# Graph network on one core: the first gather of a tile waits for the scores of the tile three places ahead, in layers 1 and 3

## Chip, cores and metric

The kernel runs on one core of one Trainium2 chip. The metric is the device time of one execution in microseconds (us), as the median of several runs. PE is TensorE, DVE VectorE, ACT ScalarE, POOL GpSimd, SP SyncE; a DMA that gathers rows is issued by POOL.

## What is computed

Four layers over a graph of N = 2048 nodes, with B = 8 batches of D = 64 features. Every layer normalises `x`, clips it at zero, lets every node attend to its neighbours in `adj`, and adds the result to `x`. Layers 1 and 3 are the ones that the change touches; both score an edge by a sum of one number of each end:

```python
def _L3_gnn_ref(x, adj, W, a):
    h = jnp.matmul(x, W)
    a1 = a[:F_out, 0]
    a2 = a[F_out:, 0]
    f1 = jnp.einsum('bnf,f->bn', h, a1)
    f2 = jnp.einsum('bnf,f->bn', h, a2)
    e = jax.nn.leaky_relu(f1[:, :, None] + f2[:, None, :], negative_slope=ALPHA)
    e = jnp.where(adj[None, :, :] > 0, e, NEG_BIG)
    attention = jax.nn.softmax(e, axis=2)
    h_prime = jnp.matmul(attention, h)
    return jax.nn.relu(h_prime)
...
    # --- layer 3 (adj_preln) ---
    h = jnp.maximum(_layernorm(x, axis=-1), 0.0)
    x = x + _L3_gnn_ref(h, adj, L3_gnn_W, L3_gnn_a)
```

Layer 1 is the same with `elu` in place of `relu` at its end. Layer 0 scores with dot products, layer 2 with dot products in two passes (four heads, then one).

## The kernel before

The graph is sparse: a node has few neighbours, and node 0 the most. In layer 0 the kernel builds edge lists from `adj`. The nodes lie in 16 tiles of 128, T0 to T15. A tile has some slots of 128 edges: `ROWS` slots in which partition p holds an edge of node p, and `PACKED` slots in which edges lie in any order and are assigned to nodes by a selection matrix on PE. Together they are 17 for T0, 8 for T1, 6 for T2, 5 for T3 to T5, 4 for T6 to T10 and 3 for T11 to T15, 81 in all.

A slot is filled by `gather(k, i, st)`: one indirect DMA from POOL takes 128 rows of `table[k]` (512 features and, in layers 1 and 3, 8 numbers `f2` behind them, 2080 bytes a row, 266 KB a slot) into one slot of `ring`, which has `RING = 26` slots of SBUF. A slot is free again when the products with it have been made. A gather thus waits for its slot of the ring, and for one of eight DMA semaphores in turn, the one that the gather eight places before it set.

`additive(k, wd, ...)` runs layer 1 (k = 1, tiles in `ORDER1`) and layer 3 (k = 4, tiles in `ORDER`). Its steps run as a pipeline over the tiles, so that a step of one tile stands beside later steps of tiles ahead of it:

- `take`: the gathers of the tile.
- `sums` (layer 3 alone): exponentials (ACT, L507) and their sums, from which a shift `fs` for each node comes.
- `first`: the scores. `by_edge` brings the node's own number to packed edges (PE), DVE adds it to the gathered number (L532, L535), `leaky` (DVE, L448) ends the scores, ACT takes the exponential (L542), DVE copies it (L544).
- `check`: `by_query` sums the weights by node (PE L399, DVE L403), `weigh_sum` multiplies the ring's slots by the weights (DVE or POOL, L380) and sums them on PE (L385); this frees the slots.
- `third`, `project` and the end: division (DVE L465), transposition (PE L306, ACT L307), product with the weight matrix (PE L561), then in layer 1 `elu` (ACT L570 and L571, DVE L572), the sum with `x` (L473), and the norm for the next layer (DVE L267 to L288, POOL L290 and L292), in layer 3 `relu` and the sum (DVE L906) and the store.

Tiles come in these orders:

```python
ORDER1 = [13, 14, 15, 12, 11, 10, 0, 7, 6, 1, 5, 2, 4, 3, 9, 8]
ORDER = [13, 12, 11, 10, 9, 8, 0, 7, 6, 1, 5, 2, 4, 3, 14, 15]
```

Semaphores are set by the framework from what instructions read and write. A scheduler at build time decides the order of the instructions on each engine from estimated times and from these dependences; on the chip, each engine then runs its own list in that order. In layer 3 all gathers stand on POOL in one row with nothing between them; in layer 1 some of the norm's instructions stand between.

Of the kernel before, what the change touches and what calls it, by code (L numbers as in the profile page):

```python
# [1 line left out]

# [11 lines left out]
OP = mybir.AluOpType  # L14
# [4 lines left out]
SLOPE = 0.2  # L19
# [15 lines left out]

PAIRS = [0, 0, 2, 2, 2, 0, 0, 0, 2, 2, 2, 2, 2, 2, 2, 2]
QE = 4


MAKING = [15, 14, 13, 0, 12, 11, 10, 1, 9, 2, 8, 3, 7, 4, 6, 5]  # L40
# [19 lines left out]
def edge_stack(ctx: ExitStack, tc: tile.TileContext, x_in, adj, w1, w1t, a1, wh, wht, bh, wo, bo,  # L60
# [9 lines left out]
    nc = tc.nc  # L70
# [52 lines left out]
    def slots(t, i):  # L123
        return t[:, OFF[i]:OFF[i] + SLOTS[i]]
# [87 lines left out]
    order = list(MAKING)  # L212

    def pipeline(*stages):

        states = {}
        for n in range(NT + len(stages) - 1):
            for s in reversed(range(len(stages))):
                if 0 <= n - s < NT:
                    i = order[n - s]  # L220
                    stages[s](i, states.setdefault(i, {}))
# [4 lines left out]
    def tiny(n):  # L226

        at = spot[0] if spot[0] + n <= F else 0
        spot[0] = at + n
        return bank[0][:, at:at + n]  # L230
# [3 lines left out]
    def rows(i, lo, hi, most=RING):  # L234

        t = lo
        while t < hi:
            at = (held[i] + t) % RING
            m = min(most, hi - t, RING - at)
            yield t, m, ring[:, at:at + m, :]  # L240
            t += m
# [1 line left out]
    def row(i, t):  # L243
        return ring[:, (held[i] + t) % RING, :F]

    def gather(k, i, st):

        n = SLOTS[i]
        assert sum(SLOTS[j] for j in held) + n <= RING
        held[i], front[0] = front[0], (front[0] + n) % RING  # L250
        cols = table[k].shape[1]
        for t in range(n):
            nc.gpsimd.indirect_dma_start(  # L253
                out=ring[:, (held[i] + t) % RING, :cols], out_offset=None, in_=table[k][:, :],
                in_offset=bass.IndirectOffsetOnAxis(ap=idx[:, OFF[i] + t:OFF[i] + t + 1], axis=0))

    def load(st, name, src, bufs):
        st[name] = rows_pool[0].tile([P, F], F32, name=name, bufs=bufs)
        nc.sync.dma_start(out=st[name], in_=src)
# [41 lines left out]
    def transposed(src):  # L301

        t = rows_pool[0].tile([P, F // P, P], F32, name="xt", bufs=3)
        p = ps_q.tile([P, F], F32, name="q")
        for k in range(F // P):
            nc.tensor.transpose(p[:, k * P:(k + 1) * P], src[:, k * P:(k + 1) * P], ident)  # L306
        nc.scalar.copy(t.rearrange("p k n -> p (k n)"), p)  # L307
        return t
# [83 lines left out]
    def by_query(i, w, cols):  # L392


        K, T = ROWS[i], PACKED[i]
        w, packed = w if isinstance(w, list) else (w[:, :K, :], w[:, K:, :])
        p = (thin[0] or ps_m).tile([P, F], F32, name="m")
        for t in range(T):
            nc.tensor.matmul(p[:, :cols], selt(i, t), packed[:, t, :], start=(t == 0), stop=(t == T - 1))  # L399
        if K == 1:  # L400
            return w[:, 0, :], p[:, :cols]
        d = small.tile([P, cols], F32, name=f"row{cols}")
        nc.vector.tensor_reduce(d, w.rearrange("p k c -> p c k"), AX.X, OP.add)  # L403
        return d, p[:, :cols]

    def by_edge(i, v, cols):

        T = PACKED[i]
        p = (thin[0] or ps_m).tile([P, F], F32, name="m")
        pv = p[:, :T * cols].rearrange("p (t c) -> p t c", t=T)  # L410
        for t in range(T):
            nc.tensor.matmul(pv[:, t, :], sel(i, t), v, start=True, stop=True)
        return pv
# [31 lines left out]
            nc.vector.tensor_tensor(dst, p, u, op=OP.max)  # L445

    def leaky(dst, src):
        nc.vector.scalar_tensor_tensor(dst, src, SLOPE, src, op0=OP.mult, op1=OP.max)  # L448


    def first0(i, st):
# [3 lines left out]
    def second(i, st, wp=None):  # L455
        w = slots(w_all, i)
        d, p = by_query(i, w, B)
        st["rec"] = small.tile([P, B], F32, name="rec")
        nc.vector.tensor_tensor(st["rec"], p, d, op=OP.add)
        nc.vector.reciprocal(st["rec"], st["rec"])  # L460
        st["y"] = weigh_sum(i, st, w) if wp is None else weigh_sum(i, st, wp, eng=nc.vector)
        done(i, st)

    def divide(st, dst):
        nc.vector.tensor_tensor(heads(dst), heads(st["y"]), wide(st["rec"]), op=OP.mult)  # L465
# [11 lines left out]
    def take0(i, st):  # L477
        gather(0, i, st)
        load(st, "rows", rows_of(0, i), 3)
# [6 lines left out]
    def both(*fs):  # L486
        def f(i, st):
            for g in fs:
                g(i, st)
        return f  # L490
# [8 lines left out]

    def additive(k, wd, *finish):  # L500
        def take(i, st):
            gather(k, i, st)

        def sums(i, st):
            w = slots(w_all, i)
            for t, m, g in rows(i, 0, SLOTS[i]):
                nc.scalar.activation(w[:, t:t + m], g[:, :, F:], AF.Exp, scale=1.0 / TEMP)  # L507
            d, p = by_query(i, w, B)
            S = small.tile([P, B], F32, name="S")
            nc.vector.tensor_tensor(S, p, d, op=OP.add)  # L510
            nc.vector.tensor_reduce(most[:, 1, i:i + 1], S, AX.X, OP.max)
            nc.vector.tensor_reduce(least[:, 1, i:i + 1], S, AX.X, OP.min)

            z = small.tile([P, B], F32, name="z")
            nc.vector.tensor_scalar(z, S.bitcast(I32), TEMP * LN2 / 2 ** 23, -127.0 * TEMP * LN2, op0=OP.mult,
                                    op1=OP.add)
            nc.vector.tensor_tensor(z, z, f1s[:, i, :], op=OP.add)
            st["fs"] = small.tile([P, 2, B], F32, name="fs")
            nc.scalar.copy(st["fs"][:, 0, :], f1s[:, i, :])
            leaky(st["fs"][:, 1, :], z)  # L520

        def first(i, st):
            K, T = ROWS[i], PACKED[i]
            w = slots(w_all, i)
            s = slots(s_all, i)
            fs = st["fs"].rearrange("p t b -> p (t b)") if k == 4 else f1s[:, i, :]
            n = 2 * B if k == 4 else B
            pr = tiny(2 * B)
            nc.vector.tensor_copy(pr[:, :n], fs)
            pv = by_edge(i, fs, n)  # L530
            for t, m, g in rows(i, 0, K):
                nc.vector.tensor_tensor(s[:, t:t + m, :], g[:, :, F:], pr[:, None, :B].to_broadcast([P, m, B]),  # L532
                                        op=OP.add)
            for t, m, g in rows(i, K, K + T):
                nc.vector.tensor_tensor(s[:, t:t + m, :], g[:, :, F:], pv[:, t - K:t - K + m, :B], op=OP.add)  # L535
            leaky(s, s)
            if k == 4:
                nc.vector.tensor_tensor(s[:, :K, :], s[:, :K, :], pr[:, None, B:].to_broadcast([P, K, B]),
                                        op=OP.subtract)
                nc.vector.tensor_tensor(s[:, K:, :], s[:, K:, :], pv[:, :, B:], op=OP.subtract)  # L540
                nc.vector.tensor_scalar(s, s, 60.0, None, op0=OP.min)
            nc.scalar.activation(w, s, AF.Exp)  # L542
            wp = tiny((K + T) * B)
            nc.vector.tensor_copy(wp, w.rearrange("p t b -> p (t b)"))  # L544
            st["wp"] = wp.rearrange("p (t b) -> p t b", b=B)

        def check(i, st):
            second(i, st, st["wp"])
            if k == 1:
                nc.vector.tensor_reduce(most[:, 0, i:i + 1], st["rec"], AX.X, OP.max)  # L550
                nc.vector.tensor_reduce(least[:, 0, i:i + 1], st["rec"], AX.X, OP.min)

        def third(i, st):
            st["att"] = rows_pool[0].tile([P, F], F32, name="att")
            divide(st, st["att"])
            st["xt"] = transposed(st["att"])

        def project(i, st):
            p = st["p"] = ps_q.tile([P, F], F32, name="q")
            for j in range(F // P):  # L560
                nc.tensor.matmul(p[:, j * P:(j + 1) * P], st["xt"][:, j, :], wd, start=True, stop=True)  # L561
            finish[0](i, st)

        mid = [sums] if k == 4 else []
        pipeline(take, *mid, first, both(check, xs_rows), third, project, *finish[1:])
# [148 lines left out]
    with tc.tile_pool(name="l2", bufs=2) as l2p, \  # L714
# [10 lines left out]
        def fetch(upto):  # L725

            while len(sent) <= min(upto, len(stream) - 1):
                i, t = stream[len(sent)]
                q = sent[i, t] = l2p.tile([P, QW], F32, name="qe", bufs=QE)
                nc.gpsimd.indirect_dma_start(  # L730
# [3 lines left out]
        def take2(i, st):  # L734
# [4 lines left out]
            else:  # L739
                st["q"] = own_pool[0].tile([P, QW], F32, name="q")  # L740
                nc.sync.dma_start(out=st["q"], in_=qtab[i * P:(i + 1) * P, :])
            fetch(stream.index((i, 0)) + min(PACKED[i], QE) - 1)

        def score(i, st, lo, hi):
# [5 lines left out]
            for t in range(lo, hi):  # L750
# [11 lines left out]
                if t >= K:  # L762
                    fetch(stream.index((i, t - K)) + QE)

# [675 lines left out]
```

## Time and profile before

| | us |
|---|---|
| median of 3 runs | 1672.45 (1670.03 to 1676.54) |
| the profiled execution | 1721.51 |
| its span, first to last instruction | 1719.7 |
| layer 1, first gather to last gather's start | 402.5 to 540.4 |
| layer 3, first gather to last gather's start | 1529.0 to 1670.2 |
| busy in the span: DVE | 1318.4 (77%) |
| busy in the span: PE | 1215.1 (71%) |
| busy in the span: POOL | 1153.4 (67%) |
| busy in the span: ACT | 744.5 (43%) |

The profiled execution took 2.9% more than the median; times inside a stage come from it alone. A line of the profile's groups has the line of the kernel, the engine and operation, output and inputs with their shapes, the count, then busy time, mean duration of one (ns), and the idle time just before with what ended it. "issue" as a releaser means that the engine waited for nothing that the profile shows, "remote" that the semaphore's sender isn't in the profile's reckoning. A timeline's line has start, duration, engine, line and operation, and in brackets the idle time before it with its releaser.

### The profile page before, as it was taken

Reading aid. Unit: us, or ns where it says so; the run is one execution under the profiler, and the core shown is the slowest. Engines: PE = TensorE matmul, PEld = TensorE weight load, DVE = VectorE, ACT = ScalarE, POOL = GpSimd, SP = SyncE. Lnnn points to the kernel's source line nnn. Section 1 sums busy time; section 2 is a strip of 40 time slices with the busy share of each in tenths; the row PEclk is TensorE's granted clock in tenths of the full one; section 3 lists DMA queues with packets and bytes.
Section 4 is the critical chain, followed back from the end, with each engine's and each line's share of the span. In section 5 each row is a group of like instructions: output and inputs, shape, how many; then the busy total and the mean of one; then the engine's idle time right before and its main releaser. Section 6 shows DMA issues by size and latency. Waiting matters only on the chain.

```text
span 1719.7 us, 15784 instructions
## 1 busy us (share of the span) xinstructions
PE 1215.1 (71%) x3771; PEld 606.6 (35%) x3771; DVE 1318.4 (77%) x2748; ACT 744.5 (43%) x2378; POOL 1153.4 (67%) x903
## 2 busy tenths in 40 slices
PE   0025667776479974599997999999467877555877
PEld 0002334443234431234342444443223433333545
DVE  6979999992469987699997899831389889823656
ACT  5841324441146783356531545545234445620011
POOL 5766867786554125898789889985577896654540
PEclk9998876896699997799999999999787879657989
DMA  5555454455566447656255345200643542235651
GB/s 172 167 182 179 152 200 153 141 198 156 147 201 235 158 179 260 233 189 208 87 201 200 113 157 177 87 13 19 255 141 99 154 146 70 81 119 164 197 170 51
DMA packets 85787, 266.94 MB, mean 155 GB/s; under 512 B 14627, under 2 KB 14659, under 8 KB 75446
## 3 DMA queue, kind: packets, MB, share of 16 engines
q0 software_dynamic: 37328, 141.05, 26.7%
q1 hardware_dynamic: 48358, 124.79, 20.4%
q8 instruction: 32, 0.52, 0.1%
q14 instruction: 69, 0.57, 0.1%
HBM read 208.74 MB, written 57.05 MB: 155 GB/s over the span
## 4 chain that ended last, share of the span: by engine, by line
PE 25%; POOL 11%; DVE 9%; issue 7%; ACT 5%; DMA 3%; another core or an unknown queue 2%; DVEq 0%; SPq 0%; POOLq 0%; ACTq 0%
PE y L787 10%; PE y L385 4%; POOL g L253 3%; POOL wh L772 3%; PE m L836 2%; ACT yn L795 2%; PE m L824 2%; PE y L779 2%; POOL wg L380 1%; DMA g<-table,idx 1%; POOL ln_r L290 1%; DMA rows<-table 1%; PE m L399 1%; DVE prod L755 1%
## 5 line engine op out<-in xcount | busy, mean ns | idle before, releaser
L253 POOL DMA_INDIRECT g<-table,idx x405 | 399.2, 986 | 233.5 <-issue 161.7
L772 POOL TENSOR_TENSOR wh<-g,w 128x1024 f32<-128x1024 f32 x162 | 307.5, 1918 | 30.0 <-PE y L787 28.0
L385 PE MATMUL y<-wg,ident 128*128 128x512 f32 x392 | 234.5, 729 | 72.7 <-POOL wg L380 64.3
L290 POOL TENSOR_TENSOR ln_r<-ln_q,mhalf 128x8 f32<-128x8 f32 x80 | 135.8, 1701 | 160.6 <-DVE ln_q L288 85.1
L759 DVE TENSOR_REDUCE s<-prod 128x32 f32<-128x2048 f32 x81 | 184.0, 2286 | 14.8 <-ACT w L761 12.9
L380 POOL TENSOR_TENSOR wg<-g,w 128x1024 f32<-128x1024 f32 (+1 forms) x91 | 158.9, 1756 | 37.3 <-ACT w L436 24.2
L787 PE MATMUL y<-wh,ident 128*128 128x512 f32 x320 | 154.6, 610 | 28.9 <-POOL wh L785 25.1
L385 PE MATMUL y<-wg,selt 128*128 128x512 f32 x256 | 141.6, 663 | 5.4 <-POOL wg L380 4.4
L385 PEld LDWEIGHTS y<-wg,ident 128*128 128x128 f32 x392 | 81.6, 228 | 162.2 <-POOL wg L380 78.9
L787 PE MATMUL y<-wh,selt 128*128 128x512 f32 x256 | 124.7, 614 | 10.4 <-POOL wh L772 10.4
L795 ACT ACTIVATE yn<-y,rec 128x64 f32<-128x64 f32 x512 | 111.2, 368 | 27.5 <-PE y L787 26.9
L755 DVE TENSOR_TENSOR prod<-q,g 128x2048 f32<-128x2048 f32 x49 | 111.5, 2276 | 5.3 <-ACT g L753 4.6
L399 PE MATMUL m<-w,selt 128*128 128x8 f32 (+1 forms) x384 | 59.5, 258 | 76.0 <-ACT w L542 38.2
L380 DVE TENSOR_TENSOR wg<-g,tiny 128x1024 f32<-128x1024 f32 (+1 forms) x92 | 98.2, 1086 | 17.1 <-PE y L385 8.8
L399 PEld LDWEIGHTS m<-w,selt 128*128 128x128 f32 x384 | 63.5, 213 | 122.3 <-ACT w L542 43.6
L442 DVE SCALAR_TENSOR_TENSOR zt<-m,bhc,att 128x512 f32<-128x512 f32 x64 | 47.3, 738 | 75.0 <-ACT att L441 74.4
L298 ACT ACTIVATE xh<-x,ln_r 128x64 f32<-128x64 f32 x256 | 88.3, 428 | 18.8 <-POOL ln_r L292 18.7
L787 PEld LDWEIGHTS y<-wh,ident 128*128 128x128 f32 x320 | 59.0, 193 | 104.9 <-issue 63.8
L428 PE MATMUL q<-rows,sel 128*128 128x512 f32 x128 | 84.3, 762 | 15.7 <-DVE prod L422 5.0
L753 ACT COPY g<-g 128x512 f32<-128x512 f32 x81 | 50.4, 622 | 100.5 <-DVE prod L755 87.9
L755 DVE TENSOR_TENSOR prod<-qe,g 128x2048 f32<-128x2048 f32 x32 | 73.0, 2282 | 17.0 <-DMA qe<-qtab,qidx 15.9
L779 PE MATMUL y<-rows,ident 128*128 128x512 f32 x128 | 70.0, 634 | 18.3 <-DMA rows<-table 13.6
(210 smaller groups left out, 2584.7 us busy)
## 6 DMA issues: line engine op xcount, KB each, us to landing
qtab<-q SPq DMA_DIRECT2D x16, 1040.0 KB
a<-in_adj_dram SPq DMA_DIRECT2D x16, 1024.0 KB
q<-qtab SPq DMA_DIRECT2D x14, 1040.0 KB
table<-xh SPq DMA_DIRECT2D x48, 256.0 KB
rows<-table SPq DMA_DIRECT2D x48, 256.0 KB
xs<-x SPq DMA_DIRECT2D x48, 256.0 KB
x<-xs SPq DMA_DIRECT2D x48, 256.0 KB
table<-xh SPq DMA_DIRECT2D x32, 260.0 KB
```

The lines of the kernel that those rows point to most:

```text
L253: nc.gpsimd.indirect_dma_start(out=ring[:, (held[i] + t) % RING, :cols], out_offset=None, in_=table[k][:, :], in_offset=bass.IndirectOffse ...
L290: nc.gpsimd.tensor_tensor(st["rstd"][:, 0, :], q, mhalf, op=OP.pow)
L298: nc.scalar.activation(dst[:, b * D:(b + 1) * D], st["src"][:, b * D:(b + 1) * D], func, bias=0.0 if st["less"] is None else r[:, 1, b:b + ...
L380: eng.tensor_tensor(wg[:, :m].rearrange("p t (b d) -> p t b d", b=B), g[:, :, :F].rearrange("p t (b d) -> p t b d", b=B), w[:, t0:t0 + m, ...
L385: nc.tensor.matmul(y, lhs(i, t), wg[:, t - t0, :], start=(t == 0 and own is None), stop=(t == n - 1))
L399: nc.tensor.matmul(p[:, :cols], selt(i, t), packed[:, t, :], start=(t == 0), stop=(t == T - 1))
L755: nc.vector.tensor_tensor(pr.rearrange("p (b h) d -> p b h d", h=H), q[:, :B * H * D].rearrange("p (b h d) -> p b h d", h=H, d=D), heads(g ...
L759: nc.vector.tensor_reduce(s[:, t - lo, :], pr, AX.X, OP.add)
L772: nc.gpsimd.tensor_tensor(wg, heads(row(i, t))[:, :, None, :].to_broadcast([P, B, 2, D]), w[:, :, 2 * k:2 * k + 2, None].to_broadcast([P, ...
L779: nc.tensor.matmul(st["ys"][j], ident, xb[:, 4 * j:4 * j + 4], start=True, stop=False)
L787: nc.tensor.matmul(st["ys"][j], lhs(i, t), wg[:, 4 * j:4 * j + 4], start=False, stop=(t == n - 1))
L795: nc.scalar.activation(yn[:, b, h, :], st["ys"][j][:, b, h, :], AF.Copy, scale=st["rec"][:, 4 * j + b, 2 * k + h:2 * k + h + 1])
```

## The change

A dictionary `taken` keeps, for each layer and tile, the instruction that ends the tile's scores (`leaky(s, s)` in `first`). `take` hands to `gather` the one of the tile three places ahead in the layer's order, and `gather` makes it a dependence with a semaphore, of the tile's first slot (t = 0) alone. The first three tiles of each layer have none. In layer 0 and layer 2 `gather` is called as before.

```diff
+SPREAD = 3
...
-    def gather(k, i, st):
+    taken = {}
+
+    def gather(k, i, st, behind=None):
...
         for t in range(n):
-            nc.gpsimd.indirect_dma_start(
+            g = nc.gpsimd.indirect_dma_start(
                 out=ring[:, (held[i] + t) % RING, :cols], out_offset=None, in_=table[k][:, :],
                 in_offset=bass.IndirectOffsetOnAxis(ap=idx[:, OFF[i] + t:OFF[i] + t + 1], axis=0))
+            if behind is not None and t == 0:
+                tc.add_manual_dep(g.ins, behind.ins.name, mybir.DependencyInfo(
+                    mybir.DependencyClass.Sync, mybir.DependencyReason.DATA), reason="gather")
...
     def leaky(dst, src):
-        nc.vector.scalar_tensor_tensor(dst, src, SLOPE, src, op0=OP.mult, op1=OP.max)
+        return nc.vector.scalar_tensor_tensor(dst, src, SLOPE, src, op0=OP.mult, op1=OP.max)
...
         def take(i, st):
-            gather(k, i, st)
+            n = order.index(i)
+            gather(k, i, st, taken[k, order[n - SPREAD]] if n >= SPREAD else None)
...
-            leaky(s, s)
+            taken[k, i] = leaky(s, s)
```

An import that nothing uses is left out here. The lines of the kernel after are shifted: by 4 at the gather (L253 becomes L257), by 7 from the norm to `leaky` (L290 becomes L297, L448 becomes L455), by 8 behind that (L507 becomes L515).

More of the change, by code (lines that the diff above doesn't have):

```diff
@@ L1 @@
-from contextlib import ExitStack
+from contextlib import ExitStack, nullcontext
 import concourse.bass as bass
```

## The prediction

> **What bounds the kernel now.** I read the page's chain and costliest groups first, then the waits of the two stages that the change touches, then their engines one by one in time.
>
> ```profile
> PE 25%; POOL 11%; DVE 9%; issue 7%; ACT 5%; DMA 3%; another core or an unknown queue 2%; DVEq 0%; SPq 0%; POOLq 0%; ACTq 0%
> L253 POOL DMA_INDIRECT g<-table,idx x405 | 399.2, 986 | 233.5 <-issue 161.7
> ```
>
> No engine holds the whole span. A gather costs POOL 0.99 us, and about 1.25 us from one start to the next (below), so the 81 gathers of a layer need 101 us. The layers last longer: layer 1 from 402.5 to about 660, layer 3 from 1529.0 to 1715. In layer 1 the stretches say what binds (columns: stretch, length, then busy time of PE, PEld, DVE, ACT, POOL, then clock, DMA share, GB/s):
>
> ```profile
> 400.00:450.00 50.00, 15.31 (x50) 8.62 (x49) 10.93 (x42) 1.25 (x4) 33.27 (x35) 0.64 0.66 187
> 450.00:500.00 50.00, 36.77 (x135) 21.33 (x136) 29.79 (x71) 18.31 (x55) 27.79 (x29) 0.85 0.55 162
> 500.00:600.00 100.00, 93.96 (x348) 49.36 (x346) 93.97 (x211) 71.61 (x199) 35.17 (x37) 1.00 0.56 199
> ```
>
> Up to 450 only POOL works hard: it issues 35 gathers in an unbroken stream. From 500 DVE and PE are 94% busy, so the layer is bound by them and not by gathers: the last gather starts at 540.4, the scores of the last tile come at 590.4. The waits of 400 to 560 tell why the start is empty (waiter, releaser, total us, times, longest):
>
> ```profile
> ACT e L570 <- remote: 44.4, 2, 29.5
> ...
> POOL g L253 <- DVE wg L380: 22.5, 4, 9.1
> POOL g L253 <- issue: 20.4, 70, 0.3
> ```
>
> ACT waited 29.5 us for a semaphore whose sender the profile can't name; in the trace it is PE's, for matmuls recorded as ended 25 us before. On POOL and DVE at that place (start, duration, what ended the idle time):
>
> ```profile
> 445.20 0.95 POOL L253 DMA_INDIRECT g<-table,idx  x1 [0.30 <-issue]
> 455.21 0.95 POOL L253 DMA_INDIRECT g<-table,idx  x1 [9.06 <-DVE wg L380]
> ```
>
> ```profile
> 434.83 0.17 DVE L448 SCALAR_TENSOR_TENSOR s<-s 128x24 f32<-128x24 f32 x1
> 452.39 0.70 DVE L572 SCALAR_TENSOR_TENSOR q<-q,e 128x512 f32<-128x512 f32 x1 [17.38 <-ACT e L571]
> ```
>
> The stream stops at 446.15 because the ring is full, PE's updates come at 451.1, and DVE goes on at 452.39. Layer 3 repeats it: the stream stops at 1568.94, and DVE goes on at 1573.45 after this wait (1525 to 1720):
>
> ```profile
> ACT w L507 <- DMA g<-table,idx: 59.6, 12, 14.5
> ...
> DVE x L906 <- remote: 13.3, 1, 13.3
> ```
>
> From then on layer 3 too runs behind its gathers: the last one starts at 1670.2, and the scores of its tile come at 1704.8.
>
> **What the skill says.** The Trainium skill, "DMA: Bandwidth & Descriptors", Anatomy of one DMA, says that DMA engines don't wait on semaphores; the wait is on the issuing sequencer. The trace agrees: POOL's own row shows the 9.06 us. So a gather that waits holds back every later gather, and every norm (L290) queued on POOL. The same page, Issuing engines are not separate DMA queues, says that DMAs from all engines share the same 16 DMA engines; a stopped gather stream thus leaves room to others. The trace shows 187 GB/s in the stream, and doesn't show anybody served sooner. "Perfetto Trace Analysis", Tensor Engine Instruction, says that TensorE's recorded end is an estimate: the 25 us between recorded end and update may therefore be work that really ended late.
>
> **The change part by part.** Both kernels have the same gathers, bytes and arithmetic. Only a tile's first slot (t = 0) gets the new wait; slots 1 and up have none, and the scheduler puts them ahead. The order of instructions on POOL shows what moves. Layer 1: slot 0 of T12 goes from gather 10 to 18, T11 13 to 21, T10 16 to 27, T0 20 to 34, T5 53 to 61, T9 74 to 80, T8 78 to 81; T7, T6 and T1 move by at most a place or two. Layer 3: T10 10 to 21, T9 14 to 27, T8 18 to 31, T0 22 to 35, T15 79 to 81. No row of before shows the waits, so I compare each with the time at which before had the scores it waits for.
>
> *New waits, layer 1.* Gather n of the stream starts at 402.5 + 1.25(n - 1). T12's first slot, gather 18, starts at 424 and needs T13's scores, there at 409.3. Gather 21 needs T14's (413.6) at 428, gather 27 T15's (418.6) at 435: no stall. Gather 34 needs T12's (434.83 before) at 443.8. Here the order on DVE matters: after, L572 of T13 with what follows it (x, the norm's sum, a division: 3 x 0.7 us) stands ahead of T12's scores, before it stood behind. L572 waits for PE's late update. So gather 34 stops the stream two gathers (2.5 us) sooner than the ring did; if PE's update follows the stop as before (5 us), L572 runs at 449.9, T12's scores at 452.5 instead of 434.83, gather 34 at 452.7.
>
> *Behind gather 34.* POOL now has T13's norm (L290) ahead of the last gather of T0. The norm ran 9.8 us after L572 before, so 459.7, takes 1.7, and the last gather of T0 starts at 461.4 instead of 455.21, lands some 3.5 us later at 465 (gathers in the trace land 3 to 4 us after issue), and T0's scores came at 469.9: hidden, with 5 us to spare. But T12's products, at 453.7 to 456.7 before, now follow two of T13's norm steps on DVE and move to about 461; T11's and T10's scores go behind them. T0's scores come 5 us later, less the 2.5 us of the earlier stop: **+3 us** for layer 1, from 0 (T13's work done earlier returns it) to +10.
>
> *Later waits, layer 1.* T7 needs T11's scores (459.0), T6 T10's (464.9), T1 T0's (469.9), where POOL had waited for ring slots until 455.2, 464.0 and 496.3 anyway: 0. T9's and T8's first slots need T2's (546.7) and T4's (557.4), though before had finished gathering at 541.4: up to 16 us late, but these tiles are scored at 582 and 590. Norms behind them on POOL ran at 546.7 and 558.2: 0 to 2 us. Cover: the lag of 50 us.
>
> *Layer 3.* Gather 21 needs T13's scores (1538.4) at 1554, gather 27 T12's (1549.7) at 1562: no stall. Gather 31 needs T11's, 1574.6 before, at 1567: the stream stops two gathers sooner than before, where gather 33 met the full ring. If PE's update follows, all moves up by 2.5 us. Gather 35 needs T10's (1584.2), where before waited until 1587.6 for the ring. DVE also loses sums of T10 to T8 that stood ahead of other tiles' scores. **-2.5 us**, from -8 to +4. At the end gather 81 waits for T4's scores (1685.7; 1670.2 before), lands near 1689.5, and is used near 1693.5: hidden by 4 us. If the tiles ahead gain time, this cover moves with them.
>
> *Other stages.* POOL, DVE and ACT have some instructions in another order in layer 2 and in the tail of its second pass. Nothing in the trace prices that. In 1310 to 1460 of that pass DVE idles 12 us of 150, which bounds a gain; I take 0, and 6 us either way. SP's transfers are the same in number and only shift among themselves: 0.
>
> Sum: +3 - 2.5 + 0 = +0.5 us on the profiled run's 1721.51, of which the span is 1719.7. That run is 49 us over the median of 1672.45, in no place I can name; I carry the difference over as it is: **1673**.
>
> **The rivals.** *No change* (0.40): the above; with the terms' bounds 1664 to 1681. A measurement here tells 0.5%, 8.4 us, from nothing.
>
> *Slower* (0.38): T0 is the ring's largest tile, and all tiles after it queue behind it. If the stop at gather 34 doesn't free PE sooner, L572 stays at 452.4 or later, and T12's scores, the norm, T0's last slot and T0's scores move one for one. It decides when T12's scores in layer 1 come after 457: T0's last gather then lands after 469.9, its cover. Price: 6 us for T12 to T10 one behind the other, plus 3 to 6 for T0; in layer 3 the three tiles whose first slot comes 11 to 13 gathers later (14 to 16 us) pay the same if they aren't lagging there. Together +9 to +25, that is 1681 to 1698. For it: DVE has nothing else to do there. Against: PE's updates followed each stop of the stream, by about 5 us.
>
> *Faster* (0.22): the waits for PE's updates sum to 29.5 + 15 us on ACT in layer 1 and 13.3 + 3.7 + 5.6 us on DVE in layer 3, 67 us; each ended 2 to 5 us after the gathers paused. If the gather stream holds PE's work up, and waits at gathers 34, 38, 41 and 45 break it more often, a sixth to a third of that goes: 1650 to 1661. Against: the longest stretch, the first, shrinks by two gathers only.
>
> *It doesn't do what it says*: with slots 1 and up free to go ahead, a tile's gathers are not spread, and only 13 of 81 move. This is part of why I expect so little, and lies in the first case.
>
> **Numbers.** 1673 is the likeliest case's. The range of 1655 to 1697 takes in most of the slower case and half of the faster one.
>
> **What would show it.** Right: in layer 1 the gather stream pauses at gather 34 for L448, T12's scores come near 452 and T0's near 473; in layer 3 the pause comes at gather 31, and L906 runs near 1571. Wrong: "remote" waits much below 67 us, or T0's scores in layer 1 past 478, or a shift of over 6 us already between the end of layer 1 and the start of layer 3.

## Result, and the profile after

| | us |
|---|---|
| before, median of 14 runs | 1672.96 (1668.29 to 1678.42) |
| after, median of 14 runs | 1666.83 (1663.42 to 1671.05) |
| ratio | 0.9966, 95% interval 0.9955 to 0.9977 |
| profiled execution of after, and its span | 1669.76, 1668.0 |

The change makes the kernel 0.34% faster, 5.7 us (the two medians stand 6.1 us apart). That is less than the 0.5% from which the prediction trusted a measurement, but the interval is clear of 1, and the prediction had the sum at +0.5 us.

**Two conditions.** The kernel before takes about 1673 us on one part of the chips and about 1723 us on others, steadily in each comparison. The first comparison and one later one (e14, e15) were at 1673, the other experiments, on four chips, at 1723; so was the profile of before that the prediction read. A profile of before at 1673 us came with e15. Beside it, the 49 us have a place (each stage from its first gather to the next stage's; "ahead" is all that stands before layer 1's first gather):

| profile | ahead | layer 1 | between | layer 3 | span |
|---|---|---|---|---|---|
| before, shown with the prediction | 402.5 | 257.1 | 869.5 | 190.7 | 1719.7 |
| before at 1673 us (e15) | 405.9 | 234.5 | 866.4 | 164.1 | 1670.8 |
| after | 406.7 | 228.5 | 872.0 | 160.8 | 1668.0 |

Between the two profiles of before, 22.6 us lie in layer 1 and 26.6 us in layer 3. Between e15 and after, layer 1 is 6.0 us shorter and layer 3 3.3 us, but the stages between are 5.6 us longer and those ahead 0.8. That makes 2.8 us, half of what the medians show; the profiled execution of after was 2.9 us over its median. The stages between spread from 866.4 to 873.2 us over all profiles of before, so this one pair says where single stretches changed, and not from which layer the 5.7 us come. The waits of after from 400 to 560 (waiter, releaser, total us, times, longest) show what has gone from these layers:

```profile
ACT w L550 <- DVE s L455: 33.1, 5, 11.2
...
POOL g L257 <- DVE s L455: 18.6, 4, 9.0
POOL g L257 <- issue: 16.1, 56, 0.3
```

No wait is "remote" here, and none in e15's profile either. In both, PE's updates come in time while the gathers stream. The new wait is there (POOL on L455, four times, 18.6 us in sum), but not where the prediction saw it. Gathers 34 and 35 of after start 1.25 us apart, with POOL's norm behind them:

```profile
448.04 0.95 POOL L257 DMA_INDIRECT g<-table,idx  x1 [0.30 <-DMA g<-table,idx]
449.29 0.95 POOL L257 DMA_INDIRECT g<-table,idx  x1 [0.31 <-issue]
450.27 1.68 POOL L297 TENSOR_TENSOR ln_r<-ln_q,mhalf 128x8 f32<-128x8 f32 x1
452.13 1.01 POOL L257 DMA_INDIRECT g<-table,idx  x1 [0.18 <-issue]
```

The four waits stand at gathers 69, 76, 80 and 81. The last two, for T9 and T8:

```profile
532.57 0.95 POOL L257 DMA_INDIRECT g<-table,idx  x1 [4.05 <-DVE s L455]
544.50 1.02 POOL L257 DMA_INDIRECT g<-table,idx  x1 [9.00 <-DVE s L455]
```

Gather 81 starts 137.8 us after the first one, in e15 115.6.

Where layer 1 gained is seen when it is cut at the end of T0's products (the end of DVE's last multiplication of T0's slots by their weights). First e15, then after (stretch, length, then busy time of PE, PEld, DVE, ACT, POOL, then clock, DMA share, GB/s):

```profile
405.90:476.70 70.80, 51.89 (x187) 30.50 (x188) 40.57 (x112) 18.92 (x57) 55.09 (x58) 0.78 0.73 214
476.70:640.40 163.70, 135.64 (x479) 69.19 (x478) 143.32 (x278) 122.96 (x339) 51.91 (x57) 0.97 0.54 196
```

```profile
406.70:480.30 73.60, 54.50 (x193) 32.42 (x194) 41.58 (x114) 20.57 (x60) 57.09 (x60) 0.78 0.75 220
480.30:635.20 154.90, 132.13 (x471) 67.07 (x469) 139.21 (x276) 121.49 (x335) 50.14 (x53) 0.98 0.54 196
```

Up to there after is 2.8 us behind; in the rest it needs 154.9 us instead of 163.7, and DVE, the busiest engine, has 4.1 us less work and 4.7 us less idle time (163.7 - 143.3 = 20.4 against 15.7). The work is not saved: DVE has 1.0 us more ahead of the cut, and in the stages between it is busy for 685.8 us instead of 682.0. DVE's waits in that rest, e15 and then after:

```profile
DVE prod L331 <- ACT q L330: 7.1, 10, 1.7
DVE ln_q L287 <- ACT ln_sq L281: 5.6, 4, 2.1
DVE att L465 <- PE q L306: 4.3, 1, 4.3
```

```profile
DVE ln_q L294 <- ACT ln_sq L288: 7.0, 6, 1.6
DVE prod L338 <- ACT q L337: 4.9, 7, 1.7
DVE att L472 <- PE q L313: 2.0, 2, 1.6
```

They are waits of the norm and of the query products for layer 2, not for gathers. DVE's order changed too: some 180 of its 390 instructions of layer 1 would have to be moved to get one trace's order from the other's. In layer 3 the waits of 1505 to the end, e15 and then after:

```profile
ACT w L507 <- DMA g<-table,idx: 80.3, 18, 14.4
POOL g L253 <- issue: 40.8, 63, 8.6
```

```profile
ACT w L515 <- DMA g<-table,idx: 75.1, 18, 14.2
...
POOL g L257 <- issue: 26.8, 56, 5.5
```

ACT waits 5 us less for gathered rows. POOL's idle time that the profile doesn't explain ("issue") is shorter, but its idle time before gathers isn't, taken together: in after, waits of 10.9 us for DVE's L518 and 7.3 us for its L523 are new. T0 is scored 1.7 us sooner and the layer is 3.3 us shorter.

The chain that ended last and the gathers in after:

```profile
PE 4%; DVE 1%; DMA 1%; ACT 0%; issue 0%; POOL 0%; ACTq 0%; DVEq 0%
L257 POOL DMA_INDIRECT g<-table,idx x405 | 396.1, 978 | 224.3 <-issue 122.9
```

A gather costs POOL what it did. This chain accounts for a small part of the span only, so I don't rank engines by it.

### The profile page after: what moved, and what is told of

Same layout as the page of the kernel before. It is cut to its first block, busy times and chain, and to the rows that moved or that the text cites. A ratio compares the mean times of both kernels' runs of the same rounds, so it can differ in the third digit from the quotient of the medians.

```text
span 1668.0 us, 15790 instructions
## 1 busy us (share of the span) xinstructions
PE 1218.2 (73%) x3771; PEld 603.3 (36%) x3771; DVE 1322.4 (79%) x2748; ACT 745.3 (45%) x2378; POOL 1152.4 (69%) x903
## 5 line engine op out<-in xcount | busy, mean ns | idle before, releaser
L257 POOL DMA_INDIRECT g<-table,idx x405 | 396.1, 978 | 224.3 <-issue 122.9
L392 PE MATMUL y<-wg,ident 128*128 128x512 f32 x392 | 239.0, 740 | 68.4 <-POOL wg L387 55.1
L297 POOL TENSOR_TENSOR ln_r<-ln_q,mhalf 128x8 f32<-128x8 f32 x80 | 136.0, 1702 | 129.4 <-DVE ln_q L295 58.9
L387 POOL TENSOR_TENSOR wg<-g,w 128x1024 f32<-128x1024 f32 (+1 forms) x91 | 160.2, 1771 | 38.8 <-ACT w L443 23.3
L795 PE MATMUL y<-wh,ident 128*128 128x512 f32 x320 | 153.9, 607 | 21.0 <-POOL wh L793 18.6
L387 DVE TENSOR_TENSOR wg<-g,tiny 128x1024 f32<-128x1024 f32 (+1 forms) x92 | 98.1, 1086 | 11.8 <-PE y L392 11.5
L449 DVE SCALAR_TENSOR_TENSOR zt<-m,bhc,att 128x512 f32<-128x512 f32 x64 | 47.1, 736 | 75.2 <-ACT att L448 75.2
L761 ACT COPY g<-g 128x512 f32<-128x512 f32 x81 | 50.4, 623 | 86.1 <-DVE prod L763 80.8
L787 PE MATMUL y<-rows,ident 128*128 128x512 f32 x128 | 70.8, 639 | 17.7 <-DMA rows<-table 12.7
L305 ACT ACTIVATE xh<-ln_xc,ln_r 128x64 f32<-128x64 f32 x256 | 65.9, 336 | 36.3 <-POOL ln_r L297 33.9
```

Of the source, the lines that this page charges most:

```text
L257: g = nc.gpsimd.indirect_dma_start(out=ring[:, (held[i] + t) % RING, :cols], out_offset=None, in_=table[k][:, :], in_offset=bass.IndirectO ...
L297: nc.gpsimd.tensor_tensor(st["rstd"][:, 0, :], q, mhalf, op=OP.pow)
L305: nc.scalar.activation(dst[:, b * D:(b + 1) * D], st["src"][:, b * D:(b + 1) * D], func, bias=0.0 if st["less"] is None else r[:, 1, b:b + ...
L387: eng.tensor_tensor(wg[:, :m].rearrange("p t (b d) -> p t b d", b=B), g[:, :, :F].rearrange("p t (b d) -> p t b d", b=B), w[:, t0:t0 + m, ...
L392: nc.tensor.matmul(y, lhs(i, t), wg[:, t - t0, :], start=(t == 0 and own is None), stop=(t == n - 1))
L795: nc.tensor.matmul(st["ys"][j], lhs(i, t), wg[:, 4 * j:4 * j + 4], start=False, stop=(t == n - 1))
```

## Experiments

Ratios are to the kernel before on the same chip. The table has the profiles' stages, in us after the first gather of the layer: when T0's products end, what then remains of the layer, when T8 (the last tile of layer 1) is scored and the tail behind that; for layer 3 T0's scores and the whole layer.

| run | ratio | T0's products | rest | T8 scored | tail | layer 1 | between | layer 3: T0 scored | layer 3 |
|---|---|---|---|---|---|---|---|---|---|
| *before 1673 us:* e15 before | | 70.8 | 163.7 | 165.7 | 68.8 | 234.5 | 866.4 | 64.9 | 164.1 |
| after | 0.9966 | 73.6 | 154.9 | 172.8 | 55.7 | 228.5 | 872.0 | 63.2 | 160.8 |
| e14 after and pause | 1.0057 | 72.2 | 164.0 | 172.2 | 64.1 | 236.2 | 881.6 | 63.4 | 163.0 |
| *before 1723 us:* e0 before | | 99.0 | 159.3 | 189.0 | 69.3 | 258.2 | 872.2 | 83.9 | 192.9 |
| e5 before | | 94.5 | 162.5 | 187.4 | 69.6 | 257.0 | 873.2 | 84.9 | 192.2 |
| e10 before | | 98.2 | 160.4 | 189.6 | 69.0 | 258.6 | 869.1 | 83.4 | 189.6 |
| e13 before | | 98.6 | 159.1 | 188.4 | 69.3 | 257.7 | 872.8 | 83.6 | 189.9 |
| e4 after | 0.9924 | 94.5 | 154.3 | 192.2 | 56.6 | 248.8 | 873.4 | 75.5 | 179.5 |
| e1 layer 1 only | 0.9943 | 95.0 | 153.5 | 192.8 | 55.8 | 248.5 | 874.8 | 81.5 | 190.1 |
| e16 the same | 0.9965 | 96.8 | 154.9 | 196.8 | 54.9 | 251.7 | 873.7 | 80.8 | 189.2 |
| e2 layer 3 only | 0.9966 | 98.1 | 159.5 | 188.5 | 69.1 | 257.6 | 871.9 | 75.2 | 183.0 |
| e17 the same | 0.9965 | 98.5 | 159.2 | 188.3 | 69.4 | 257.7 | 872.0 | 75.8 | 181.5 |
| e3 order, no wait | 1.0055 | 98.4 | 164.7 | 195.5 | 67.6 | 263.1 | 874.9 | 78.3 | 187.0 |
| e6 all slots | 0.9899 | 81.3 | 161.5 | 180.6 | 62.3 | 242.8 | 867.5 | 79.6 | 183.8 |
| e7 norms earlier | 1.0020 | 97.8 | 164.2 | 204.7 | 57.2 | 262.0 | 869.5 | 80.5 | 192.3 |
| e8 layer 3, early | 0.9983 | 98.9 | 159.1 | 188.7 | 69.3 | 258.0 | 872.4 | 74.0 | 184.5 |
| e9 all slots in layer 1 | 0.9867 | 86.1 | 161.2 | 185.3 | 62.0 | 247.3 | 869.8 | 72.7 | 183.5 |
| e11 one pause | 0.9954 | 88.4 | 160.2 | 178.8 | 69.7 | 248.6 | 872.6 | 81.7 | 186.4 |
| e12 one pause each | 1.0022 | 88.3 | 160.1 | 178.8 | 69.5 | 248.4 | 873.9 | 93.0 | 202.1 |

### The kernel before, profiled again (e0, e5, e10, e13, e15)

No edit.

> The kernel before, unchanged, profiled a second time. If the 49 us that its first profile had over its median belong to that one execution, this profile's span is near 1671 us, the remote waits of layers 1 and 3 (67 us in sum) are mostly gone, and layer 1 and layer 3 together are some 45 us shorter than in the first profile. If profiling this kernel always costs it 49 us, the remote waits come again at the same places.

> The kernel before, unchanged, for a profile to lay beside that of after. If it runs at 1673 us, it has no remote waits to speak of, and the stage times say where the 5.7 us are: theory A, all in layer 3 (1507.2 to the end took after 160.8 us, so some 166.5 here, and layer 1's 228.5 us the same); theory B, all in layer 1 (234 here). At 1724 us, it repeats the first two profiles: 258 us for layer 1 and 190 for layer 3.

> The kernel before, unchanged, for a profile beside these. Near 1673 us it has no late updates of PE's and layer 1 takes some 234 us, near 1723 it has them and takes 257.

> The kernel before, unchanged, for a profile on this call's chip. Near 1673 us: layer 1 some 234 us, with 159 to 160 us after T0's products and 74 ahead of their end, against 154.9 and 73.6 of after's first profile; then the 5.7 us of the first comparison are the stretch behind T0's products. Near 1723 us: the fifth profile with late updates.

> The kernel before, unchanged, for a profile on this call's chip. Near 1673 us: layer 1 some 234 us, with 159 to 162 us behind T0's products. Near 1723 us: it repeats the others, layer 1 at 257 to 259.

Profiling isn't the cause of the 49 us: on the chips of e0, e5, e10 and e13 the timed median of before is 1723 to 1724 us too. There the late updates return every time; e0's ACT:

```profile
452.03 0.60 ACT L570 ACTIVATE e<-q 128x512 f32<-128x512 f32 x1 [28.22 <-remote]
```

e0's gather stream made its last issue at 445.76; PE's update came at 452.0. In the profiles on chips of this kind, the update that ended the longest wait of a stream came 5 to 6 us after the stream's last gather. Four of them: 445.20 and 451.07 (the profile shown with the prediction), 448.31 and 454.39 (e2), and in layer 3 1565.27 and 1570.49 (e4), 1569.02 and 1574.51 (e5). Not every late update needs a stop. In the profile shown with the prediction, one came at 434.28, with the stream running on to 446:

```profile
434.30 0.17 DVE L535 TENSOR_TENSOR s<-g,m 128x16 f32<-128x16 f32 x1 [8.21 <-remote]
```

At 1673 us, layer 1 has longer streams and no late update: in e15 POOL never stands still for over 0.6 us between two gathers until gather 71, in after until gather 66. The pages differ in one more way: those at 1673 us give times from issue to landing of DMAs, those at 1723 us give none. Semaphore events may be missing from the latter, which makes the releasers named in them less sure. What makes the chips differ, the runs don't say.

### Each layer's part by itself (e1, e16, e2, e17), and the whole (e4)

```diff
-            gather(k, i, st, taken[k, order[n - SPREAD]] if n >= SPREAD else None)
+            gather(k, i, st, taken[k, order[n - SPREAD]] if n >= SPREAD and k == 1 else None)
```

`k == 4` in e2 and e17; e4 is the changed kernel as it is.

> The new dependence in layer 1 alone; layer 3 as before. The change gave 0.34% (5.7 us). Theory A, the gain is layer 3's: ratio 1.000 to before. Theory B, it is layer 1's (first slots held back, the gather stream stopped earlier): ratio 0.9966. If both layers share it: near 0.998. My prediction's terms (+3 in layer 1, -2.5 in layer 3) would give 1.002.

> The dependence in layer 1 alone, as in e1. Where before takes 1673 us, one profile of each kernel has layer 1 at 234.5 us in before and 228.5 in the change, with all of it behind T0's products. If that is the 0.34%: ratio 0.9965. Where before takes 1723 us: 0.994 again.

> The new dependence in layer 3 alone; layer 1 as before. Theory A: 0.9966. Theory B: 1.000. If both layers share it: near 0.998. My prediction's term for layer 3 alone, -2.5 us: 0.9985.

> The dependence in layer 3 alone, as in e2. Where before takes 1673 us, layer 3 is 164.1 us in before's profile and 160.8 in the change's: 0.998 if that holds, 1.000 if the gain is layer 1's alone. Where before takes 1723 us: 0.9966 again.

> The changed kernel, unchanged, beside the kernel before. Where before takes some 1724 us, with waits for late updates of PE's at the gather streams of layers 1 and 3, layer 1 alone gave 0.9943 and layer 3 alone 0.9966; if the two add, after is at 0.991 there. Where before takes 1673 us, as in the first comparison, it is 0.9966 again, with hardly a remote wait.

All on chips where before takes 1723 us. Layer 1 alone: 0.9943 (0.9922 to 0.9964) and 0.9965 (0.9951 to 0.9979). Layer 3 alone: 0.9966 (0.9951 to 0.9981) and 0.9965 (0.9952 to 0.9979). Both: 0.9924 (0.9905 to 0.9943). Within their intervals the two parts add, and both layers have a gain there. In layer 1 the rest behind T0's products is 153.5 to 154.9 us in e1, e4, e16 and in after's own profile, and 159.1 to 163.7 in every profile of before: this part doesn't need late updates. Its means are 154.4 and 160.7. In layer 3 T0's scores come 8 us sooner than in before, at 75 instead of 84 us; at 1673 us this is 1.7.

### The order of the gathers without the waits (e3)

```diff
-                    mybir.DependencyClass.Sync, mybir.DependencyReason.DATA), reason="gather")
+                    mybir.DependencyClass.NoSync, mybir.DependencyReason.DATA), reason="gather")
```

> The dependence is kept for the scheduler only, with no semaphore: POOL issues the gathers in exactly the changed order, but none waits for scores. If the order of gathers (and what the scheduler makes of it on the other engines) brings the gain, the ratio to before is again near 0.9966. If the waits do it, by holding the gather stream back, it is 1.000 or over. DVE, ACT and PE come out in an order that is neither that of before nor that of after, so 2 us either way prove nothing.

1.0055 (1.0037 to 1.0073). No gather waits for scores here, but the stream stops all the same. Behind gather 35 POOL waits 13.29 us for T13's norm, which stands ahead of gather 36, and ACT's late update comes in that pause (a wait of 30.3 us):

```profile
445.74 0.95 POOL L257 DMA_INDIRECT g<-table,idx  x1 [0.30 <-issue]
459.98 1.67 POOL L297 TENSOR_TENSOR ln_r<-ln_q,mhalf 128x8 f32<-128x8 f32 x1 [13.29 <-DVE ln_q L295]
```

Layer 1 is 5 us longer than before's. The order of DVE is a third one: of its 2748 instructions, some 500 would have to be moved to get after's order, and some 600 to get before's. So the run shows that a kernel with the first slots put back and no waits can lose; it doesn't separate the waits from the order.

### All slots wait (e6, e9)

```diff
-            if behind is not None and t == 0:
+            if behind is not None:
```

e9 has `if behind is not None and (k == 1 or t == 0):`, so that layer 3 is as in the change.

> All slots of a tile depend on the scores of the tile three ahead, not the first alone, in both layers. POOL then issues the gathers in the order of before, and the stream really stops: in layer 1 gather 10 waits for T13's scores, and gather 20, T0's first, for T12's. If holding the stream back is what helps, this is at least as fast as after: ratio to before 0.99 or less. If the late landing of tiles costs more, it is slower than before: T0's 17 gathers start at T12's scores, some 10 us after they started in before, and land that much later, in each of two layers: 1.01.

> All slots of a tile wait in layer 1 (243 us there in that run, 249 in the changed kernel), the first slot alone in layer 3 (180 us, against 184). If the two layers are independent: 0.989, a little below all slots in both (0.9899).

0.9899 (0.9881 to 0.9917) and 0.9867 (0.9853 to 0.9882), the fastest run at 1723 us. With the gathers in before's order and real stops, T0's products end at 81 and 86 us instead of 94 to 99, and the remote wait of ACT's L578 in layer 1 is down from 28 to 31 us to 9.3 and 5.1. The rest behind T0's products is 161 us, as in before: this gain lies in another place than the change's. It isn't shown to be the stops' alone, since some 470 of DVE's instructions stand in another order than in before, too.

### One pause (e11, e12)

```diff
-            if behind is not None and t == 0:
+            if behind is not None:
...
-            gather(k, i, st, taken[k, order[n - SPREAD]] if n >= SPREAD else None)
+            gather(k, i, st, taken[k, order[n - SPREAD]] if i == 0 and k == 1 else None)
```

e12 has `i == 0` without `k == 1`.

> The kernel before with the dependence at one place only: in layer 1 all 17 slots of T0 wait for T12's scores; the gathers keep the order of before. With all slots of all tiles waiting, the first stream of layer 1 stopped 4.4 us ahead of gather 20, the 28 to 31 us remote wait was gone, and T0's products ended 81 us after the layer's start instead of 98. If the pause itself frees PE's late updates, this one pause does the same: no remote wait in layer 1, T0's products at 81 to 86 us, layer 1 some 12 us shorter, ratio 0.993. If the waits of the later tiles are needed, or the order that the scheduler makes of them: 1.000. At a chip where before takes 1673 us there is nothing to free, and it is 1.000 too.

> The same one pause in layer 3 too: all slots of T0 wait for the scores of T10, three ahead. If pauses free PE's updates in both layers: 0.987, 12 us in layer 1 and 10 in layer 3. But in layer 3 T10's scores were late themselves (55 us after the start), so T0's gathers may come too late: then only e11's ratio, or worse.

e11: 0.9954 (0.9942 to 0.9966). POOL stops once, ahead of gather 20, for 3.85 us:

```profile
425.30 0.95 POOL L257 DMA_INDIRECT g<-table,idx  x1 [0.30 <-issue]
430.10 0.95 POOL L257 DMA_INDIRECT g<-table,idx  x1 [3.85 <-DVE s L455]
```

ACT's 28 to 31 us wait is gone; L578 runs during the pause, after 6.6 us:

```profile
429.17 0.60 ACT L578 ACTIVATE e<-q 128x512 f32<-128x512 f32 x1 [6.57 <-PE y L392]
```

T0's products end 6 to 11 us sooner than in before, though T0's first gather starts 3.5 us later after the layer's start than in the profile shown with the prediction. That is the pause at work and nothing else: in the traces the instructions of PE, DVE, ACT and POOL stand in exactly the order of before, by operation, tiles and shapes. The rest is before's too (160 us). e12: 1.0022 (1.0009 to 1.0036). The same pause in layer 3 lasts almost five times as long, since the scores that it waits for were late themselves, and layer 3 takes 202 us (the profile names another step of DVE's, close in time, as the releaser):

```profile
1551.07 0.95 POOL L257 DMA_INDIRECT g<-table,idx  x1 [0.31 <-issue]
1570.34 0.95 POOL L257 DMA_INDIRECT g<-table,idx  x1 [18.32 <-DVE z L523]
```

### Layer 3's early tiles (e8)

```diff
-            gather(k, i, st, taken[k, order[n - SPREAD]] if n >= SPREAD else None)
+            gather(k, i, st, taken[k, order[n - SPREAD]] if n >= SPREAD and k == 4 and n <= 6 else None)
```

> The dependence in layer 3 alone, and there for T10, T9, T8 and T0 only. Layer 3 alone gave 0.9966, with T0's scores 8.5 us sooner after the layer's start. If the stop of the first stream is what helps, this has all of it: 0.9966, T0's scores 75 us after the start. If the later waits do part of it, it is nearer to 0.999.

0.9983 (0.9971 to 0.9995), T0's scores at 74.0 us. In between: the early waits bring T0's scores all the way forward, but behind T0 layer 3 takes 110 us (184.5 - 74.0), against 106 to 108 in e2 and e17 and 106 to 109 in before. The intervals of e8, e2 and e17 overlap, so how much the later waits add isn't shown.

### DVE's order alone (e7)

```diff
-            leaky(s, s)
+            lk = leaky(s, s)
+            n = order.index(i)
+            if k == 1 and n >= 14:
+                tc.add_manual_dep(lk.ins, ended[order[n - 4]].ins.name, mybir.DependencyInfo(
+                    mybir.DependencyClass.NoSync, mybir.DependencyReason.DATA), reason="order")
...
-        nc.vector.scalar_tensor_tensor(p, p, 0.0, e, op0=OP.max, op1=OP.add)
+        ended[i] = nc.vector.scalar_tensor_tensor(p, p, 0.0, e, op0=OP.max, op1=OP.add)
```

> The kernel before with two ordering edges on DVE and nothing else: in layer 1 the scores of T9 and T8 stand behind the elu steps of T5 and T2 (each four places ahead), as they do in the changed kernel. Gathers, their order and their waits are those of before. In the profiles so far, 6 tiles had their elu step still ahead of them after the last scores in before, 4 in after, and that tail of layer 1 took 69 and 56 us, while T8's scores came only 4 us later. Theory C, layer 1's gain is this order on DVE: tail near 56 us, layer 1 8 us shorter, ratio to before 0.995. Theory B, the held-back gathers themselves bring it: ratio 1.000.

This is an edit of before; `leaky` returns its instruction as in the change, and `ended` is a new dictionary. The two edges moved more than they name: the scheduler put some 290 instructions of DVE, 290 of PE and 280 of ACT in other places.

1.0020 (1.0009 to 1.0030). The tail is as short as the change's, 57.2 us, but T8's scores come 16 us later. Theory C falls in this form: work put ahead of the last scores only pushes them back. In the change they come 4 to 8 us later for the same 13 us. There, work of tiles far ahead moved too: T12's elu step, for one, stands ahead of T7's scores in after and behind them in before. Whether that makes the difference, no run shows.

### The change and the pause (e14)

```diff
-            if behind is not None and t == 0:
+            if behind is not None and (t == 0 or k == 1 and i == 0):
```

> The changed kernel, with one thing more: in layer 1 all slots of T0 wait for T12's scores, not the first alone. One pause alone brought T0's products to 88 us after the layer's start where before had 98 and the change 94.5; the change alone brought the stretch behind them to 154 us, where the pause alone left it at 160. If the two are separate gains and add: layer 1 at 242 us against 257 in before, layer 3 near 180 as in the change, ratio 0.985. If the scheduler's order for the one undoes the other: 0.99.

1.0057 (1.0040 to 1.0075), where before takes 1673.59 us. There is no late update to free there, the rest of layer 1 is back at 164 us, and the stages between take 881.6 us. No wait of the edit stands in these, so the 15 us more than in e15 are put down to the scheduler's order; some 5 us may be this one execution's, which was that much over its median. So the fastest kernels at 1723 us can't be called better in general: e6 and e9 were not run where before takes 1673.

## Why the prediction was wrong

**The profile's 49 us.** The step that carried the difference between profile and median over "as it is" failed. The 49 us had a place, layers 1 and 3 with their late updates, and the timed runs, by e15's and after's profiles, had none of them. All that was built on the late updates, the stop two gathers sooner and L572 waiting for it, doesn't exist where the time was predicted; remote waits much below 67 us were the sign that I had named for this. Where it exists, the picture holds: in e4 gather 34 stops the stream for L455, L580 runs late, T12's scores follow.

```profile
446.86 0.94 POOL L257 DMA_INDIRECT g<-table,idx  x1 [0.30 <-issue]
457.11 0.94 POOL L257 DMA_INDIRECT g<-table,idx  x1 [9.31 <-DVE s L455]
```

```profile
453.81 0.70 DVE L580 SCALAR_TENSOR_TENSOR q<-q,e 128x512 f32<-128x512 f32 x1 [13.29 <-ACT e L579]
456.66 0.18 DVE L455 SCALAR_TENSOR_TENSOR s<-s 128x24 f32<-128x24 f32 x1
```

T12's scores come 50.0 us after the layer's start there (predicted 50.0) and T0's 68.3 (predicted 70.5).

**Layer 1 up to T0, +3 us.** Measured +2.8 in the two profiles at 1673 us. The size is right, and the path is not: T12's first slot, gather 18, starts near 428 and T12 is scored at 433.7 (27.0 us after the start; e15: 19.6). It is late by its own place in the stream, 10 us further back than in e15. The prediction asked only whether gather 18 stalls, and not how late it comes. Of T12's 7.4 us, 1.2 are left at T0's scores.

**Later waits, layer 1: 0.** This is the term that failed: the prediction gave it 0, at most +2 us, and the rest of layer 1 went from 163.7 to 154.9 us, -8.8. The means of the four profiles with the change's layer 1 and the six of before differ by 6 us. I read 94% busy DVE as no room, and costed only the waits, not what the scheduler does with the other engines: I named order changes in layer 2 and in its second pass, and overlooked them in layer 1 itself, where DVE's 20 us of idle time and the 69 us tail were open to them. Part is given back, under the term for other stages (0, 6 us either way): in the four profiles with layer 1 changed and layer 3's waits or not (after, e1, e4, e16) the stages between average 873.5 us, in the six of before (the one shown with the prediction among them) 870.5. Two of the query products that e15 makes ahead of layer 2's first gather are made behind it in after (58 against 56). In the pair at 1673 us nearly all is given back (6.0 and 5.6 us), so what layer 1 adds to the 5.7 us there stays open; at 1723 us e1 and e16 show a gain of the layer by itself.

**Layer 3, -2.5 us.** Measured -3.3 at 1673 us, where the reason that I gave (a late update freed by a sooner stop) doesn't apply: near the right number, by luck. At 1723 us it is -8 to -12 (e2, e17 and e4 against a mean of 191 in before), and the reason can apply. In e4 POOL does pause ahead of gather 31, and DVE's L914 goes on at 1570.51 in that pause (predicted: near 1571). The term had a fifth to a third of the size. The stretch ended with T0's scores 8 us sooner, not 2.5.

**The faster rival** was right of the 1723 us chips in that a pause frees PE's updates (e11), and there the change gains 0.76%. But the change itself leaves ACT's long wait in place (27.4 us in e4), so its gain there isn't shown to be this one. At 1673 us the rival has nothing to work on. **That the change doesn't do what it says** holds in part: slots 1 and up go ahead, and no gather before the 69th stands still for scores in layer 1 of after. All slots waiting (e6) makes other stops and, at 1723 us, a faster kernel.

**The bounds.** The terms' own bounds sum to -14 and +22 us, that is 1658 to 1694; the 1664 to 1681 given for them is the 0.5% either way.

What stays open: whether the rest of layer 1 is shorter because of the waits on the chip or because of the order that the scheduler gave DVE, ACT and PE. e3 and e7 each bring an order of their own and get neither; a run with after's whole order and no wait wasn't made. Which layer the 5.7 us at 1673 us come from stays open too: the runs with one layer changed were all at 1723 us.

## What to carry to other kernels

When a profile's own time is 3% over the median of the timed runs, find those 3% first, in a second profile if need be: costs read from stalls that the timed runs don't have are costs of another machine. Where a scheduler orders the instructions, a new dependence is a new order for every engine in its stage, and its effect may lie there and not at the wait. An engine that is 94% busy in a stretch can have room in the stage it belongs to (DVE's 20 us in the rest of layer 1); compare whole stretches, cut at the same event, before a term is set to zero. And add up all stages before a gain is put down to one: what leaves a stage can come back in the next.

## What the runs showed that I had not expected

On four of the chips PE's semaphore updates came late while gathers streamed from POOL, and those that ended the longest waits came 5 to 6 us after the stream's last issue; the kernel then takes 1723 us instead of 1673, with 22.6 us of the difference in layer 1 and 26.6 in layer 3. A pause of 3.85 us in the stream, with no other change of order, brought layer 1 from 258 to 249 us there (e11). A gather costs POOL 0.98 to 0.99 us under both conditions, so the stream itself looks alike, and the profile doesn't name the cause.
